# Cross attention over 256 keys: the tail of one more quad deferred, one copy reordered, one batch's loads a slot later

## The chip, the core and the metric

The kernel runs on one core of one Trainium2 chip. The metric is the device time of one execution in microseconds (us). All times below are of the kernel before the change, unless said otherwise.

## The reference

Eight batches of 256 tokens, 1024 features, 32 heads of 32. `x` is normalised, projected to queries, attends to 256 context rows that serve as keys and values without a projection, and the result is projected and added to `x`:

```python
mu, var = mean(x), var(x)                          # over the 1024 features
xn = (x - mu) * rsqrt(var + 1e-5) * ln_gamma + ln_beta
Q = split_heads(xn @ Wq.T)                         # (8, 32, 256, 32)
K = V = split_heads(ctx)                           # (8, 32, 256, 32)
probs = softmax(where(mask, Q @ K.T * 32**-0.5, -inf))
out = x + merge_heads(probs @ V) @ Wout.T
```

All arithmetic is in 32-bit floats.

## The kernel before

The work is cut into 64 **quads**: a quad is four heads of one batch, so quad n is heads 4(n % 8) to 4(n % 8) + 3 of batch n // 8. The main loop (L905) has one **slot** n per quad. In slot n TensorE (PE) does, in this order: the scores of quad n + 1 (`scores`, L471, 16 matmuls), the weighted sum of values of quad n - 2 (`values`, L614, 64 small matmuls), query projections for quads to come (`make_q`, L331, into one PSUM bank; from slot 18 on `query_product`), and steps of the output projection of the batch before (`product_steps`, L681). The order of all this is written out by hand: instructions are issued to every engine in program order.

`softmax_parts` (L491), called in slot n for quad n + 1, does the softmax of four heads. `exps(j)` takes minimum and exponential of head j (VectorE, then ScalarE), `normalize(j)` divides (VectorE and GpSimd), `blocks(j)` transposes 32 x 32 blocks into the tile `pT` (VectorE), and `aside` copies parts of `pT` to `pc` (ScalarE). What is left then is the **tail** (L595): `blocks(3)`, `aside(1)`, two transfers `pT<-pT` of 128 KB (L600), then the loads listed in `between`, and then two transfers `pT<-pc` (L604). The last two overwrite what the first two read, so each waits for the landing of its partner. `values` of the quad needs all four. The tail is either issued at once or put in the list `tails`; then the next softmax issues it behind its own `exps(0)` (L555). L608 decides which: quads below 8, and quads 57 to 62, are put in the list.

All these transfers go through SyncE's queue (SP), which issues them in program order; an issue takes 0.5 to 0.6 us. Each carries one of eight completion semaphores in turn (100 to 105, 107 and 108 in the trace's operands) and waits, before it is issued, until the transfer eight places earlier has landed.

Behind the softmax, slot n issues the rest of its list: layer norm steps, and `move_x` (L316 to L327), which carries the normalised and block-transposed `x` of a batch from tile `xe` to tile `xnT` in sixteen transfers of 64 KB. For batch 2 the moves lie in slots 5 (four), 6 (six) and 7 (six), and the first reader is `make_q` of quad 16 in slot 10.

The table of slots (L790 to L816): for batch 3 (`SPLIT`), `first` is 18, so its `x` is loaded (two halves of 512 KB) in the lists of slots 5 and 6, its statistics (`ln_stats`, L216) lie in slots 8 and 9, its normalisation in 10 and 11. A load in the list of slot n goes out with the tail of quad n + 1. Statistics of slots up to 8 are used to fill gaps in the softmax; later ones come behind it.

Before the main loop, quad 0 is done by hand (L851 to L882): its query projection in two halves of tokens, `first_q(0)` and `first_q(1)` (each eight chunks of matmuls and one ScalarE copy, L289), the scores of each half, and `softmax_parts(0, ...)` as a generator that is advanced between them.

Of the kernel before, what the change touches and what calls it, by code (L numbers as in the profile page):

```python
# [59 lines left out]
def xattn_kernel(  # L60
# [16 lines left out]
    NQ = NC  # L77
    NH = P // HD
# [8 lines left out]
    N = B * NQ  # L87
# [191 lines left out]
    def first_q(s, chunks=range(NC)):  # L279

        if s == 0:
            pqs[0] = ps_q.tile([P, 512], F32, tag="pq", name="pq_0")
        cols = ds(0, P) if s == 0 else ds(P, P + 1)
        for c in chunks:
            nc.tensor.matmul(
                pqs[0][:, cols], wq[:, 0, c, :], xnT0[:, c, cols],
                start=(c == chunks[0]), stop=(c == chunks[-1]),
            )
        nc.scalar.activation(qa[:, 0, cols], pqs[0][:, cols], AF.Copy, scale=NEG_SCALE)  # L289
# [83 lines left out]
    SPLIT = 3  # L373
# [110 lines left out]
    def softmax(*args):  # L484
        for _ in softmax_parts(*args):
            pass
# [4 lines left out]
    def softmax_parts(n, copies=(), ahead=(), between=(), hooks={}, fill=()):  # L491

        fill = list(fill)

        def fill_in():
            if fill:  # L500
                fill.pop(0)()

        pss = scs[n]
        pT = pTs[n] = ptp.tile([P, 2, NI, NH, NS, K], F32, tag="pT", name=f"pT_{n}")
        pc = asp.tile([P, NI, NH, NS, K], F32, tag="pc", name=f"pc_{n}")
        es, mns, dens = {}, {}, {}

        def exps(j, part=range(NS)):
            if 0 in part:
                es[j] = ep.tile([P, NS, T], F32, tag="e", name=f"e_{n}_{j}")  # L510
                mns[j] = sm.tile([P, NS], F32, tag="mn", name=f"mn_{n}_{j}")
                dens[j] = sm.tile([P, NS], F32, tag="den", name=f"den_{n}_{j}")
            e, mn, den = es[j], mns[j], dens[j]
            for s in part:
                nc.vector.tensor_tensor_reduce(  # L515
                    out=e[:, s, :], in0=pss[j][:, s, :], in1=mbs[n // NQ], scale=1.0,
                    scalar=NO_SCORE, op0=ALU.add, op1=ALU.min, accum_out=mn[:, s : s + 1],
                )
                nc.scalar.activation(  # L519
                    e[:, s, :], e[:, s, :], AF.Exp, bias=mn[:, s : s + 1], scale=-1.0,  # L520
                    accum_out=den[:, s : s + 1],
                )

        def normalize(j):
            rden = sm.tile([P, NS], F32, tag="rden", name=f"rden_{n}_{j}")
            nc.vector.reciprocal(rden, dens[j])  # L526
            for s in range(NS):
                nc.gpsimd.tensor_scalar(  # L528
                    es[j][:, s, :], es[j][:, s, :], rden[:, s : s + 1], 1.0,
                    ALU.mult, ALU.mult,  # L530
                )

        def blocks(j):
            nc.vector.transpose(  # L534
                pT[:, :, :, j, :, :].rearrange("p a i s k -> p (a i) s k"),
                es[j].rearrange("p s (b t) -> p b s t", t=K),
            )

        def aside(j):
            nc.scalar.copy(pc[:, :, ts(j, 2)], pT[:, 1, :, ts(j, 2)])  # L540

        if n == 0:
            for j in range(NH - 1):
                exps(j, (0,))
            yield
            exps(NH - 1, (0,))
            fill_in()
            yield
            for j in range(NH):
                exps(j, (1,))  # L550
            normalize(0)
            fill_in()
        else:
            exps(0)
            while tails:  # L555
                tails.pop()()
            late = "p1" in hooks
            if not late:
                for done in list(pvs):
                    copy_at(done)  # L560
            exps(1)
            for hook in hooks.get("soon", ()):
                hook()
            exps(2)
            normalize(0)
            for hook in hooks.get("p1", ()):
                hook()
            exps(3)
            if late:
                for done in list(pvs):  # L570
                    copy_at(done)
        copies = list(copies)
        for copy in copies[: NQ if n <= NQ else 1 if n == NQ + 1 else 0]:
            copies.remove(copy)
            copy()
        for hook in hooks.get(0, ()):
            hook()
        normalize(1)
        fill_in()
        blocks(0)  # L580
        for hook in hooks.get(1, ()):
            hook()
        normalize(2)
        fill_in()
        blocks(1)
        aside(0)
        normalize(3)
        fill_in()
        blocks(2)
        while fill:  # L590
            fill_in()
        for copy in copies:
            copy()

        def tail():  # L595
            blocks(3)
            aside(1)

            for r in range(2):
                nc.sync.dma_start(pT[ts(2 * r, K), 1], pT[ts(2 * r + 1, K), 0])  # L600
            for load in between:
                load()
            for r in range(2):
                nc.sync.dma_start(pT[ts(2 * r + 1, K), 0], pc[ts(2 * r, K)])  # L604

        for load in ahead:
            load()
        if n < NQ or N - NQ < n < N - 1:  # L608
            tails.append(tail)
        else:  # L610
            tail()
        yield
# [16 lines left out]
    def copy_at(n):  # L629
        b, c = divmod(n, NQ)  # L630
        k, c = divmod(c, NK)
        if c == 0:
            ats[b, k] = atp.tile([P, NK, NS, NA, K], F32, tag="at", name=f"at_{b}_{k}")
        for r, pv in enumerate(pvs.pop(n)):
            nc.scalar.copy(  # L635
                ats[b, k][:, c, :, ts(r, 2), :], pv.rearrange("p a s k -> p s a k")
            )
# [136 lines left out]
    for n in range(N):  # L774
# [12 lines left out]
    loads, stats, norms, trans, moves, biases, masks = (  # L787
        {n: [] for n in range(N)} for _ in range(7)
    )
    for b in range(1, B):  # L790
        first = NQ * (b - 1) + 2
        if b == 1:
            when = dict(moves=())
        elif b == 2:
            when = dict(
                loads=(0, 1), stats=(2, 3), norms=(3, 3), trans=(4, 5),
                moves=tuple(5 + (i + 2) // 6 for i in range(16)),
            )
        else:
            when = dict(  # L800
                loads=(first - 13, first - 12),
                stats=(first - 10, first - 9) if b == SPLIT else (first - 11, first - 9),
                norms=(first - 8, first - 7), trans=(first - 7, first - 6),
                moves=tuple(first - 6 + (i + 2) // 6 for i in range(16)),
            )
        for table, key in (
            (loads, "loads"), (stats, "stats"), (norms, "norms"), (trans, "trans"),
        ):
            for i, n in enumerate(when.get(key, ())):
                assert n < first  # L810
                table[n].append((b, i))
        for n in range(N):
            part = [i for i, slot in enumerate(when["moves"]) if slot == n]
            if part:
                assert n < first - 1
                moves[n].append((b, part))  # L816
        biases[NQ * b - 2].append(b)
        if b % 2 == 0:
            masks[NQ * b - 7].append(b)
# [47 lines left out]
    for c in range(NC):  # L867
        copy_x0(1, c, nc.scalar if c < NC // 2 else nc.vector)
    first = softmax_parts(0, (partial(copy_q, 1), partial(copy_q, 2)), (), (), {}, [
        partial(ln_stats, 1, 0), partial(ln_stats, 1, 1),  # L870
        partial(ln_norm, 1, 0, nc.vector),
    ])
    next(first)
    first_q(1)
    make_q(1, second=True, chunks=range(2))
    next(first)
# [9 lines left out]
    for b in range(B - 1):  # L886
        done, ends = 0, b == B - 2
        for i, counts in enumerate(ENDS if ends else STEPS):
            n = NQ * (b + 1) + i
# [15 lines left out]
    for n in range(N):  # L905
        b, i = divmod(n - NQ, NQ)
# [222 lines left out]
```

## Time and profile before

| | us |
|---|---|
| median of 3 runs | 575.77 (575.03 to 577.52) |
| the profiled execution, its own time | 575.24 |
| its span, first to last instruction | 573.5 |
| PE busy in it | 565.9 (99%), granted clock 0.999 |
| VectorE (DVE), ScalarE (ACT), GpSimd (POOL) busy | 459.2, 412.3, 403.8 (80%, 72%, 70%) |
| transfers: bytes moved, mean rate | 117.98 MB, 206 GB/s |

The slots around the change, with the start of their scores on PE as borders (busy us of each engine, and the mean busy share of the 16 DMA engines):

| slot | from, to | length | PE | DVE | ACT | POOL | DMA |
|---|---|---|---|---|---|---|---|
| 6 | 65.30, 73.33 | 8.03 | 8.03 | 6.88 | 6.80 | 7.70 | 0.95 |
| 7 | 73.33, 80.87 | 7.54 | 7.54 | 6.79 | 6.37 | 7.45 | 0.81 |
| 8 | 80.87, 89.68 | 8.81 | 7.96 | 8.07 | 6.76 | 8.15 | 0.78 |
| 9 | 89.68, 98.24 | 8.56 | 8.56 | 5.71 | 6.66 | 7.61 | 0.77 |
| 10 | 98.24, 109.04 | 10.80 | 8.69 | 8.67 | 6.87 | 9.61 | 0.60 |
| 11 | 109.04, 118.29 | 9.25 | 9.25 | 7.08 | 6.96 | 6.13 | 0.86 |

In the profile's lines, times are us from the span's start; a line of the timeline gives start, length, engine, line of the kernel, operation, output <- inputs, shapes and count, and in brackets how long the engine was idle before and what ended that.

### The profile page before, as it was taken

What the parts mean: (1) busy time and instruction counts of PE and PEld (TensorE: products, weight loads), DVE (VectorE), ACT (ScalarE), POOL (GpSimd) and SP (SyncE); (2) the same over time, 40 slices, a digit from 0 to 9 for tenths busy, and PEclk for the clock granted to TensorE, in tenths of its full rate; (3) what the DMA queues carried; (4) which work ended last, traced back from release to release, by engine and by line L of the source; (5) the groups of instructions that cost most, each with busy time, mean ns of one, the idle gap of its engine ahead of it and who ended that gap; (6) DMA issues with size and microseconds to landing.
All of it is one profiled execution on the core that took longest, in us unless ns stands there. A gap on an engine that the chain in (4) does not pass through costs nothing.

```text
span 573.5 us, 20000 instructions
## 1 busy us (share of the span) xinstructions
PE 565.9 (99%) x7162; PEld 392.1 (68%) x7162; DVE 459.2 (80%) x1698; ACT 412.3 (72%) x1424; POOL 403.8 (70%) x675
## 2 busy tenths in 40 slices
PE   8999999899999999999999999999999999999997
PEld 8788876566667677677676677667766777755444
DVE  6897987788877879888888888888877868879823
ACT  4688886767758867698667967769767876869920
POOL 1788898789896896776567675666657667448780
PEclk9999999999999999999999999999999999999999
DMA  8675877766678667877787767886768774536751
GB/s 299 238 201 189 241 216 216 240 186 189 192 239 273 195 181 220 248 241 204 202 239 208 214 196 192 251 263 190 181 177 258 210 228 141 142 101 180 212 162 74
DMA packets 47475, 117.98 MB, mean 206 GB/s; under 512 B 9104, under 2 KB 9872, under 8 KB 47376
## 3 DMA queue, kind: packets, MB, share of 16 engines
q1 hardware_dynamic: 47088, 116.69, 68.9%
q8 instruction: 57, 0.93, 0.7%
q14 instruction: 42, 0.34, 0.2%
q10 hardware_dynamic: 288, 0.01, 0.0%
HBM read 65.28 MB, written 11.53 MB: 134 GB/s over the span
## 4 chain that ended last, share of the span: by engine, by line
PE 86%; POOL 4%; DVE 4%; DMA 2%; ACT 1%; issue 1%; SPq 1%; DVEq 0%; ACTq 0%; POOLq 0%
PE po_S L694 20%; PE pq_A L440 16%; PE pv L622 11%; PE sc L479 10%; PE po_A L694 10%; PE pq L340 7%; PE pq_S L440 6%; PE po_end L761 3%; POOL e L528 3%; DVE e L515 2%; DMA pT<-pT 1%; PE po_last L761 1%; ACT e L519 1%; PE busy L120 1%; DVE pT L534 1%
## 5 line engine op out<-in xcount | busy, mean ns | idle before, releaser
L528 POOL TENSOR_SCALAR e<-e,rden 128x256 f32<-128x256 f32 x512 | 235.8, 478 | 128.7 <-DVE rden L526 127.0
L519 ACT ACTIVATE e<-e,mn 128x256 f32<-128x256 f32 x512 | 254.1, 501 | 51.2 <-DVE mn L515 50.8
L534 DVE STREAM_TRANSPOSE pT<-e 128x512 f32<-128x512 f32 x256 | 180.7, 707 | 53.1 <-POOL e L528 35.5
L515 DVE CUSTOM_DVE_ANT_0 e<-sc,mb 128x256 f32<-128x256 f32 x512 | 185.9, 416 | 26.9 <-PE sc L479 26.4
L540 ACT COPY pc<-pT 128x512 f32<-128x512 f32 x128 | 79.0, 617 | 68.7 <-DVE pT L534 41.2
L519 ACT ACTIVATION_READ_ACCUMULATOR e<-e,mn 128x1 f32 x512 | 97.9, 191 | 0.0
L340 PE MATMUL pq<-xnT,wq 128*128 128x256 f32 (+1 forms) x368 | 84.2, 383 | 2.1 <-DMA xnT<-xe 2.1
L340 PEld LDWEIGHTS pq<-xnT,wq 128*128 128x128 f32 x368 | 68.6, 190 | 16.8 <-issue 6.9
L622 PE MATMUL pv<-pT,v 64*32 64x128 f32 x4096 | 74.8, 274 | 1.0 <-issue 0.8
L622 PEld LDWEIGHTS pv<-pT,v 64*32 64x32 f32 x4096 | 57.1, 105 | 26.7 <-issue 12.7
L479 PEld LDWEIGHTS sc<-k,qa 32*128 32x128 f32 x1024 | 46.2, 184 | 42.4 <-issue 23.2
L694 PE MATMUL po_S<-wo,at 128*128 128x512 f32 x152 | 74.3, 606 | 0.0
L479 PE MATMUL sc<-k,qa 32*128 32x256 f32 x1024 | 73.6, 400 | 0.1
L694 PE MATMUL po_A<-wo,at 128*128 128x512 f32 x128 | 60.9, 609 | 0.0
L694 PE MATMUL po_S<-wo,s 128*128 128x512 f32 x104 | 50.1, 606 | 0.0
L526 DVE RECIPROCAL rden<-den 128x2 f32<-128x2 f32 x256 | 37.6, 147 | 6.0 <-ACT e L519 4.8
L515 DVE DVE_READ_ACCUMULATOR2_ANT mn<- 128x1 f32 x512 | 42.4, 83 | 0.0
L440 PEld LDWEIGHTS pq_A<-xnT,wq 128*128 128x128 f32 x320 | 37.3, 192 | 4.8 <-issue 4.1
L694 PEld LDWEIGHTS po_A<-wo,at 128*128 128x128 f32 x128 | 22.5, 189 | 24.6 <-issue 22.7
L694 PEld LDWEIGHTS po_S<-wo,at 128*128 128x128 f32 x152 | 25.8, 190 | 19.8 <-issue 19.1
L440 PE MATMUL pq_A<-xnT,wq 128*128 128x128 f32 x320 | 37.3, 275 | 0.0
L635 ACT COPY at<-pv 128x128 f32<-128x128 f32 x128 | 26.2, 254 | 8.2 <-PE pv L622 8.2
(95 smaller groups left out, 605.1 us busy)
## 6 DMA issues: line engine op xcount, KB each, us to landing
v<-in_kv_dram SPq DMA_DIRECT2D x32, 512.0 KB, 4.4
pT<-pT SPq DMA_DIRECT2D x128, 128.0 KB, 2.9
pT<-pc SPq DMA_DIRECT2D x128, 128.0 KB, 4.1
ring<-kept_T SPq DMA_DIRECT2D x18, 512.0 KB, 5.3
k<-in_kv_dram SPq DMA_DIRECT2D x32, 256.0 KB, 3.7
x<-in_x_dram SPq DMA_DIRECT2D x14, 512.0 KB, 5.6
r<-in_x_dram SPq DMA_DIRECT2D x28, 256.0 KB, 5.1
out_dram<-r SPq DMA_DIRECT2D x28, 256.0 KB, 2.5
```

Source lines behind the costliest of these rows:

```text
L340: nc.tensor.matmul(pqs[n], wq[:, o, c, :], xnTs[b](c), start=(c == 0), stop=(c == NC - 1),)
L440: nc.tensor.matmul(pqs[b][:, o, :], w[:, c], x_[:, c], start=begins and o + c == 0, stop=c == NK - 1, skip_group_check=True,)
L479: nc.tensor.matmul(scs[n][j][:, s, :], qa[r, n % NQ, ts(s, P)], ks[n - n % 2][r, n % 2, :], start=True, stop=True,)
L515: nc.vector.tensor_tensor_reduce(out=e[:, s, :], in0=pss[j][:, s, :], in1=mbs[n // NQ], scale=1.0, scalar=NO_SCORE, op0=ALU.add, op1=ALU.m ...
L519: nc.scalar.activation(e[:, s, :], e[:, s, :], AF.Exp, bias=mn[:, s : s + 1], scale=-1.0, accum_out=den[:, s : s + 1],)
L526: nc.vector.reciprocal(rden, dens[j])
L528: nc.gpsimd.tensor_scalar(es[j][:, s, :], es[j][:, s, :], rden[:, s : s + 1], 1.0, ALU.mult, ALU.mult,)
L534: nc.vector.transpose(pT[:, :, :, j, :, :].rearrange("p a i s k -> p (a i) s k"), es[j].rearrange("p s (b t) -> p b s t", t=K),)
L540: nc.scalar.copy(pc[:, :, ts(j, 2)], pT[:, 1, :, ts(j, 2)])
L622: nc.tensor.matmul(pvs[n][r][j * HD : (j + 1) * HD], vs[n - n % 2][ts(r, 2 * K), i, ds(n % 2 * P + j * HD, HD)], pT[ts(r, 2 * K), :, i, j, ...
L635: nc.scalar.copy(ats[b, k][:, c, :, ts(r, 2), :], pv.rearrange("p a s k -> p s a k"))
L694: nc.tensor.matmul(po, operand(b, name)[:, c], wo[:, which, c], start=begins and c == 0, stop=c == NK - 1, skip_group_check=not begins,)
```

## The change

Three edits.

- In `softmax_parts` for quad 0, all four heads' first halves are now issued in one part, and the caller no longer advances the generator before `first_q(1)`. So `first_q(1)`, whose ScalarE copy was issued behind three exponentials, and the two first chunks of `make_q(1)` are now issued ahead of all four.
- L608: `n < NQ` becomes `n <= NQ` (NQ is 8). The tail of quad 8 is issued within the softmax of quad 9, behind its `exps(0)`. What slot 7 has behind the softmax, the last six moves of batch 2 among it, is thereby issued ahead of this tail.
- Batch 3's `x` goes from the lists of slots 5 and 6 into those of 6 and 7, and its statistics from slots 8 and 9 to 9 and 10.

```diff
         if n == 0:
-            for j in range(NH - 1):
+            for j in range(NH):
                 exps(j, (0,))
-            yield
-            exps(NH - 1, (0,))
             fill_in()
             yield
...
-        if n < NQ or N - NQ < n < N - 1:
+        if n <= NQ or N - NQ < n < N - 1:
             tails.append(tail)
...
             when = dict(
-                loads=(first - 13, first - 12),
-                stats=(first - 10, first - 9) if b == SPLIT else (first - 11, first - 9),
+                loads=(first - 12, first - 11) if b == SPLIT else (first - 13, first - 12),
+                stats=(first - 9, first - 8) if b == SPLIT else (first - 11, first - 9),
                 norms=(first - 8, first - 7), trans=(first - 7, first - 6),
...
-    next(first)
     first_q(1)
     make_q(1, second=True, chunks=range(2))
     next(first)
```

## The prediction

> **What bounds the kernel now.** I read the page's first part, then who PE waits for, then PE's timeline slot by slot, then SP's, since the waits left on PE lead to transfers. The page and PE's waits:
>
> ```profile
> span 573.5 us, 20000 instructions
> PE 565.9 (99%) x7162; PEld 392.1 (68%) x7162; DVE 459.2 (80%) x1698; ACT 412.3 (72%) x1424; POOL 403.8 (70%) x675
> ...
> PE pq L340 <- DMA xnT<-xe: 2.1, 1, 2.1
> PE busy L120 <- POOL ring masks.py:199: 1.3, 1, 1.3
> PE pv L622 <- issue: 0.8, 2, 0.6
> ```
>
> PE is busy 99% of the span at full clock, and its waits are few and each in one place. So no edit to another engine's order can bring more than the sum of PE's few waits. PE's timeline gives their places (slots 7 to 10; a row is a block of matmuls, its first number its start):
>
> ```profile
> 73.33 1.15 PE L479 MATMUL sc<-k,qa 32*128 32x256 f32 x16
> 74.41 1.16 PE L622 MATMUL pv<-pT,v 64*32 64x128 f32 x64
> 75.49 5.45 PE L340 MATMUL pq<-xnT,wq 128*128 128x256 f32 x24
> 80.87 1.15 PE L479 MATMUL sc<-k,qa 32*128 32x256 f32 x16
> 82.58 0.38 PE L622 MATMUL pv<-pT,v 64*32 64x128 f32 x2 [0.57 <-issue]
> 83.24 1.13 PE L622 MATMUL pv<-pT,v 64*32 64x128 f32 x62 [0.28 <-issue]
> 84.30 5.45 PE L340 MATMUL pq<-xnT,wq 128*128 128x256 f32 x24
> 89.68 1.15 PE L479 MATMUL sc<-k,qa 32*128 32x256 f32 x16
> ...
> 99.32 1.22 PE L622 MATMUL pv<-pT,v 64*32 64x128 f32 x64
> 100.47 1.12 PE L694 MATMUL po_A<-wo,at 128*128 128x512 f32 x2
> 103.70 3.69 PE L340 MATMUL pq<-xnT,wq 128*128 128x256 f32 x16 [2.11 <-DMA xnT<-xe]
> ```
>
> Slots 7 and 8 hold the same 104 matmuls, yet one takes 80.87 - 73.33 = 7.54 us and the other 89.68 - 80.87 = 8.81. The difference, **1.27 us**, lies around the values of quad 6: two of them start at 82.58, the rest only at 83.24. In slot 10, the two projection matmuls of 100.47 need 0.95 (half of the 1.81 that four take between 107.23 and 109.04), but the queries of quad 16 start at 103.70: 103.70 - 101.42 = **2.28 us**, put down to the moves of batch 2.
>
> SP's queue says why (one row: so many transfers, first issue, time until the last was issued):
>
> ```profile
> 74.53 0.44 SPq L130 DMA_DIRECT2D x<-in_x_dram  x1
> 75.02 0.43 SPq L173 DMA_DIRECT2D wo<-in_woT_dram  x1
> 75.55 1.15 SPq L604 DMA_DIRECT2D pT<-pc  x2
> ...
> 85.06 0.44 SPq L130 DMA_DIRECT2D x<-in_x_dram  x1
> 85.55 0.43 SPq L173 DMA_DIRECT2D wo<-in_woT_dram  x1
> ...
> 88.57 0.57 SPq L144 DMA_DIRECT2D v<-in_kv_dram  x1
> 94.61 1.95 SPq L604 DMA_DIRECT2D pT<-pc  x2
> 96.61 3.75 SPq L327 DMA_DIRECT2D xnT<-xe  x6
> ```
>
> Quad 6's two `pT<-pc` go out at 75.55 and land at 82.50 and 83.15 by the trace's landing records: 7 us, because the loads of v (lands 77.88), x (79.44) and wo (82.18) are ahead. PE's two starts, 82.58 and 83.24, stand just behind. The last six moves go out only from 96.61 because quad 8's tail is ahead of them, whose `pT<-pc` waits on SP until 94.61 for its partner's landing.
>
> **The change, part by part.** The sum is against the profiled execution's 575.24.
>
> (A) Without x in quad 6's tail, its `pT<-pc` no longer have 512 KB ahead that took 79.44 - 77.88 = 1.56 us. They land at 80.94 and 81.59, and the values of quad 6 can start at 80.87 + 1.08 = 81.95 (as 74.41 stands to 73.33). The wait goes: **-1.27**. It is close (0.36): if wo took the 3.0 that one took behind a k load earlier (67.50 to 70.50) instead of 2.74, 0.1 would be left; if the loads do not close up, all stays. Bounds -1.27 to 0.
>
> (B) The six moves of slot 7 come ahead of quad 8's tail, about ten us earlier. Their reader at 101.42 less 1.27 finds them landed: **-2.28**. Bounds -2.28 and -2.1, the two readings.
>
> (C) What is late next is quad 8's tail itself. On SP it now stands behind the six moves, and gets the second half of x between its two pairs. VectorE's `blocks(3)` and ScalarE's `aside(1)` go behind the `exps(0)` of quad 9, some 1 us (two exponentials of 0.50): SP reaches their reader much later, so this costs nothing. Step by step: SP gives each transfer one of eight semaphores and waits for the landing eight places back. Eight places ahead of the sixth move stands the wo load of 85.55, which lands at 93.16 now, and at 91.6 if everything from (A) on is 1.56 earlier. So that move goes out at 91.6, and behind it at SP's pace of 0.6: `pT<-pT` at 92.2 and 92.8, v 93.4, x 94.0, r 94.5, `pT<-pc` 95.0 and 95.6. The v load needs 3.9 from its issue in a short queue (3.8 and 4.0 in two answers): 97.3; x 1.56 more: 98.9; r 0.66 (96.06 to 96.72 now): 99.5; the two copies some 0.3 each: 100.1. The values of quad 8 were due at 99.32 - 1.27 = 98.05. A new wait of **+2.05**, on PE ahead of the projection and of quad 16's queries, so all of PE stands behind it. No row shows this arrangement, so bounds: low, the wo load lands when most of its engines have it (91.43 now, 1.7 ahead of the last) and the loads follow at the 1.27 of the opening's 512 KB weights: 97.8, no wait, 0. High, nothing closes up and wo lands at 93.16, and one engine is held by a 1.1 us instruction fetch as at 95.11: 102.8, +4.7. I take 2.05, nearer the low end, since its terms are those of the very neighbours.
>
> Here a rule may be held against the rows. A lone 128 KB pair transfer takes 2.3 us from issue to landing, and 512 KB in a queue 1.56. The Trainium skill ("DMA: Bandwidth & Descriptors", section "Anatomy of one DMA") gives, for the other path of issue, a fixed 2.0 us plus bytes over 436 GB/s. By it the 1.5 MB from 93.4 on would be down at 98.9, an estimate from that page, and the sum 1.2 lower; the rows say slower, and I go by them.
>
> (D) The opening. The copy of quad 0's second half of queries starts at 14.73, behind three exponentials, and the scores at 15.04 wait for it (PE's weight loads 0.49). Its last matmul ends at 14.09, so it can start at 14.15 and PE, which ends its two chunks at 14.80, gains 0.25. In exchange ScalarE holds the four exponentials, the first now at 13.24, until 14.41; four of 0.495 end the issue at 16.39 where the next is free at 16.25: 0.14 late, under a later gap of 3.09 on ScalarE before 22.08. PE's 0.25 are lost again at 26.63, where the transposes of batch 1 start as GpSimd's normalisation (22.85, 3.78 long) ends; that chain hangs on VectorE, whose order is the same. **0**, bounds -0.3 and +0.2 (without that cover, 0.14 of exponentials reach quad 0's reciprocals).
>
> (E) The statistics moved, 2 x 0.67 + 0.20 + 0.15 = 1.7 us of VectorE, leave slot 8 (8.07 busy) and come to slot 10, behind its softmax. They end by 8.7 of work in a slot over 8.5 long and only delay the next `exps(0)`, whose scores buffers PE needs a slot later: **0**, bounds 0 and +0.5. Quad 7's values start at 94.38, its copies land at 93.59 and 94.09: both move by 1.3 to 1.6, cost 0, and up to 0.6 if only PE moves.
>
> Sum: 575.24 - 1.27 - 2.28 + 2.05 = **573.74**. The median shown is 0.53 above that execution, so the forecast for a median is **574.3**.
>
> **The rivals.**
>
> *The whole gain.* Quad 8's copies land by 98.05, and both waits go for nothing: 575.77 - 3.55 = 572.2. For it: the straggling engine is 1.7 of wo's landing, and the DMA share is 0.60 in slot 10. Against: three loads of 1.28 MB between the pairs.
>
> *Slower.* The wait of quad 8's values takes over both: at the high end of (C), 575.77 - 3.55 + 4.7 = 576.9. It decides against the change once the second `pT<-pc` lands after 98.05 + 3.55 = 101.6. Quad 9's tail follows on SP, and if its values in slot 11 wait 2 us as well, it is 578.9. For it: eight transfers in flight, and SP stands still until a wo load of 7.6 us is down. Against: (A) frees that load earlier.
>
> *The x load does not do what it says.* wo is the load ahead that matters, quad 6's copies stay late, (A) is 0, and (C) starts from 93.16: 101.7 - 99.32 = 2.4 against 2.28. 575.9, no change.
>
> **How the numbers follow.** Forecast 0.52 (573.2 to 575.4), whole gain 0.22, slower 0.15, no effect of x 0.11. Low end: the whole gain less the opening's bound, 572.0; high end 577.0, the slower case. A measurement here tells about 0.5%, 2.9 us: below 572.9 or above 578.7. Faster than that 0.20 (nearly all of the whole gain), slower 0.08 (the slower case with quad 9's wait), within 0.72.
>
> **What would show it.** (A) slot 8 is 7.5 long. (B) no wait of PE for the moves; they are issued by 92. (C) the values of quad 8 wait some 2 us, its copies land near 100. (D) the copy of 14.73 at 14.2, the transposes at 26.6 as before. (E) no PE wait in slots 11 and 12. I am wrong if quad 8's copies land by 98, or after 101.6.

## The result, and the profile after

| | median of the runs, us | lowest, highest | runs |
|---|---|---|---|
| before | 575.74 | 573.01, 577.75 | 20 |
| after | 578.90 | 574.86, 581.80 | 20 |

The ratio is 1.0047, 95% interval 1.0031 to 1.0063 (the two medians alone give 1.0055): the change makes the kernel slower by 0.3 to 0.6%. Two later executions of before that took 950 us at a granted clock of 0.56 are left out of all figures below. The profiled execution of after took 574.86 us (span 573.1), less than that of before (575.24). It is the fastest of the 20, and its mean granted clock is 1.000; 12 of the others have 0.994 or less, seven 0.997. In a span of 575 us, 0.997 and 0.994 are 3.4 and 6.8 us at half clock. So the first trace of after shows the change's steps, and not yet where the typical execution loses its time. Both belong to the explanation.

First the trace of after. Who PE waits for:

```profile
PE pv L620 <- DMA pT<-pT: 2.5, 1, 2.5
PE busy L120 <- POOL ring masks.py:199: 1.4, 1, 1.4
PE pq L285 <- ACT xnT L275: 0.9, 1, 0.9
PE px L266 <- DVE x L252: 0.2, 1, 0.2
```

The waits for quad 6's values and for the moves are gone, and one new wait is there: the values of quad 8 (line 622 is 620 now). The last two rows lie in the first 9 us; the kernel with x alone moved has such a wait too (0.9), and at slot 7 this trace is 0.17 behind before's (73.50 against 73.33). PE's timeline of slots 8 to 10:

```profile
81.04 1.15 PE L479 MATMUL sc<-k,qa 32*128 32x256 f32 x16
82.11 1.22 PE L620 MATMUL pv<-pT,v 64*32 64x128 f32 x64
83.26 5.45 PE L340 MATMUL pq<-xnT,wq 128*128 128x256 f32 x24
88.64 1.15 PE L479 MATMUL sc<-k,qa 32*128 32x256 f32 x16
...
97.20 1.15 PE L479 MATMUL sc<-k,qa 32*128 32x256 f32 x16
100.83 1.52 PE L620 MATMUL pv<-pT,v 64*32 64x128 f32 x64 [2.48 <-DMA pT<-pT]
102.28 1.13 PE L692 MATMUL po_A<-wo,at 128*128 128x512 f32 x2
103.25 3.62 PE L340 MATMUL pq<-xnT,wq 128*128 128x256 f32 x16
106.70 1.88 PE L692 MATMUL po_S<-wo,s 128*128 128x512 f32 x4
108.51 1.15 PE L479 MATMUL sc<-k,qa 32*128 32x256 f32 x16
```

Slot 8 is 7.60 long (8.81 before), and the queries of quad 16 follow the projection without a gap. Slot 10 is 11.31 long (10.80 before): if the 2.28 for the moves are gone, quad 8's values cost 2.79 (2.48 of them the wait ahead of their first matmuls). SP's queue (first issue of a row, time until its last) has the order that the change gives it:

```profile
84.20 1.15 SPq L602 DMA_DIRECT2D pT<-pc  x2
85.40 6.07 SPq L327 DMA_DIRECT2D xnT<-xe  x6
91.58 1.16 SPq L598 DMA_DIRECT2D pT<-pT  x2
92.78 0.58 SPq L144 DMA_DIRECT2D v<-in_kv_dram  x1
93.40 0.45 SPq L130 DMA_DIRECT2D x<-in_x_dram  x1
93.89 1.20 SPq L150 DMA_DIRECT2D r<-in_x_dram  x1
95.19 1.61 SPq L602 DMA_DIRECT2D pT<-pc  x2
```

The sixth move goes out at 90.96, when the wo load of 83.67 has landed (90.94), and quad 8's tail behind it. Its two last copies land at 100.49 and 101.13 by the landing records; PE starts on the first at 100.83.

### The profile page after: what moved, and what is told of

Read it like the earlier page. It is cut to its first block, busy times and chain, and to the rows that moved or that the text cites. A ratio compares the mean times of both kernels' runs of the same rounds, so it can differ in the third digit from the quotient of the medians.

```text
span 573.1 us, 19993 instructions
## 1 busy us (share of the span) xinstructions
PE 565.2 (99%) x7162; PEld 391.4 (68%) x7162; DVE 459.6 (80%) x1698; ACT 412.1 (72%) x1424; POOL 403.8 (70%) x675
## 4 chain that ended last, share of the span: by engine, by line
PE 85%; POOL 5%; DVE 4%; DMA 2%; ACT 2%; issue 1%; SPq 1%; ACTq 0%; POOLq 0%
PE po_S L692 20%; PE pq_A L440 16%; PE pv L620 11%; PE sc L479 10%; PE po_A L692 10%; PE pq L340 7%; PE pq_S L440 6%; POOL e L528 3%; PE po_end L759 3%; DVE e L515 1%; DMA pT<-pT 1%; PE po_last L759 1%; ACT e L519 1%; DVE pT L534 1%; DVE st L226 1%
```

## The experiments

**After once more, and each edit alone.** These four ran on one chip (before there: 576.42, 35 runs).

> The changed kernel again. Theory 'clock': the new wait of PE for quad 8's copies (2.5 us in the profile of after) is long enough that the granted clock halves for some us behind it in most executions: median near 578.7, most executions with a mean clock of 0.994 to 0.997, and if the profiled one is such, its matmuls run at half pace somewhere in 98 to 112 us and nowhere else. Rival 'opening': the half pace lies in the first 30 us. Rival 'transfers': clock 0.999 to 1.000 throughout, and the wait itself is 5 to 7 us.

Measured: 578.79, ratio 1.005 (1.0027 to 1.0072); of its 12 executions one at clock 1.000 (575.27), three at 0.997, eight at 0.994. The profiled one (span 579.7) is of the common kind. PE's timeline of slot 10, and three stretches of it (length, busy time of PE, PEld, DVE, ACT, POOL, then the granted clock, DMA share and GB/s):

```profile
97.88 1.15 PE L479 MATMUL sc<-k,qa 32*128 32x256 f32 x16
105.33 2.08 PE L620 MATMUL pv<-pT,v 64*32 64x128 f32 x64 [6.30 <-DMA pT<-pc]
107.33 2.07 PE L692 MATMUL po_A<-wo,at 128*128 128x512 f32 x2
109.20 4.36 PE L340 MATMUL pq<-xnT,wq 128*128 128x256 f32 x16
113.39 1.88 PE L692 MATMUL po_S<-wo,s 128*128 128x512 f32 x4
115.20 1.15 PE L479 MATMUL sc<-k,qa 32*128 32x256 f32 x16
```

```profile
88.00:103.87 15.87, 11.02 (x116) 5.70 (x115) 10.75 (x40) 9.49 (x31) 13.33 (x19) 1.00 0.87 219
103.87:110.70 6.83, 5.38 (x70) 3.72 (x71) 1.25 (x4) 1.55 (x7) 0.00 (x0) 0.50 0.48 110
110.70:125.00 14.30, 14.30 (x131) 9.54 (x134) 12.49 (x44) 10.79 (x34) 12.16 (x23) 1.00 0.75 242
```

Both theories hold, each for a part. The wait is 6.30 instead of 2.48, and the clock stands at half from 103.87 to 110.70: the values' 64 matmuls take 2.00 to the next start instead of 1.45, the two projection matmuls 1.87 instead of 0.97. The spans differ by 6.6: 3.82 for the longer wait (105.33 - 97.88 against 100.83 - 97.20), 2.19 for the half clock (115.20 - 105.33 against 108.51 - 100.83), and 0.68 from ahead of slot 10. From its first rise at 4.88 (4.51 in after) to 103.87 the clock is full: the opening is not the place.

> Only the tail of quad 8 deferred. x stays in slots 5 and 6, so quad 6's wait (1.27) stays, the wait for the moves (2.28) goes, and quad 8's copies have 512 KB less ahead: a wait of 0.5 to 1.0. 'Clock': no wait reaches 2 us, so clocks of 0.999 and more, 574.0 to 574.8, about 0.998 of before. 'Opening': the same. 'Transfers': a wait of 2 us or more stays in slot 10, 575.5 to 577.

```diff
-        if n < NQ or N - NQ < n < N - 1:
+        if n <= NQ or N - NQ < n < N - 1:
```

Measured: 577.42, ratio 1.0026 (1.0004 to 1.0049); ten of 12 executions below 0.999. Above all three bands. The profiled execution (span 578.2) has lost nothing to the moves, 0.78 to quad 8's values, 1.05 to quad 5's, and 3.1 to quad 6's values, which x in the lists of slots 5 and 6 holds up as before, only longer; the clock stands at half for 3.41 us behind that.

```profile
85.62 0.38 PE L622 MATMUL pv<-pT,v 64*32 64x128 f32 x2 [1.56 <-ACT e L519]
87.56 1.57 PE L622 MATMUL pv<-pT,v 64*32 64x128 f32 x62 [1.57 <-issue]
```

So the deferral alone is a loss, just clear of noise, though it removes the wait for the moves. Where it loses, this trace does not show: quad 6's copies go out at 77.40 and 78.01, and the first transfers that the deferral puts in another place only at 90.89.

> Only the opening reordered. 'Clock' and 'transfers': as before, 575.7, ratio 0.999 to 1.001. 'Opening': 577.5 to 579, ratio 1.003 to 1.006, with a lower mean clock than the kernel before on the same chip.

```diff
-            for j in range(NH - 1):
+            for j in range(NH):
                 exps(j, (0,))
-            yield
-            exps(NH - 1, (0,))
...
-    next(first)
     first_q(1)
```

Measured: 576.68, ratio 1.0011 (0.999 to 1.0032). The opening does nothing that can be told. Its trace shows something else: it has the kernel before's wait for the moves, and here the clock falls behind it.

```profile
103.84 5.38 PE L340 MATMUL pq<-xnT,wq 128*128 128x256 f32 x16 [2.14 <-DMA xnT<-xe]
```

```profile
105.02:108.43 3.41, 3.41 (x10) 2.70 (x9) 2.88 (x6) 1.30 (x5) 3.41 (x8) 0.50 0.81 224
```

The queries of quad 16 take 5.38 instead of 3.69, after nearly the same wait as in before's trace (2.11, no fall). The kernel before has such executions too: of the 91 that ran beside these experiments, 47 have a clock of 0.999 or more (median 575.71), 41 about 0.997 (577.18).

> Only batch 3's x a slot later. Quad 6's wait goes (-1.27); the second half of x now stands in quad 8's tail ahead of its copies, and behind them the six moves: PE's wait for the moves grows from 2.28 to 4 to 5 us. 'Clock': one wait of over 2.5 us, mean clocks below 0.998, 577 to 580. 'Opening': clocks as before, 575.7 to 577. 'Transfers': 576 to 577, clock 0.999.

```diff
-                loads=(first - 13, first - 12),
-                stats=(first - 10, first - 9) if b == SPLIT else (first - 11, first - 9),
+                loads=(first - 12, first - 11) if b == SPLIT else (first - 13, first - 12),
+                stats=(first - 9, first - 8) if b == SPLIT else (first - 11, first - 9),
```

Measured: 572.96, ratio 0.9955 (0.9934 to 0.9976), 11 of 12 executions at clock 0.999 or more. All theories were wrong, that of the clock the most (577 to 580): it is the fastest of the four. PE's slot 10 and SP's queue in its trace:

```profile
97.18 1.15 PE L479 MATMUL sc<-k,qa 32*128 32x256 f32 x16
98.26 1.48 PE L622 MATMUL pv<-pT,v 64*32 64x128 f32 x64
99.66 1.12 PE L694 MATMUL po_A<-wo,at 128*128 128x512 f32 x2
100.62 3.62 PE L340 MATMUL pq<-xnT,wq 128*128 128x256 f32 x16
```

```profile
84.33 1.15 SPq L604 DMA_DIRECT2D pT<-pc  x2
85.58 1.18 SPq L600 DMA_DIRECT2D pT<-pT  x2
86.81 0.58 SPq L144 DMA_DIRECT2D v<-in_kv_dram  x1
87.43 0.46 SPq L130 DMA_DIRECT2D x<-in_x_dram  x1
87.93 0.54 SPq L150 DMA_DIRECT2D r<-in_x_dram  x1
93.01 1.15 SPq L604 DMA_DIRECT2D pT<-pc  x2
94.21 4.56 SPq L327 DMA_DIRECT2D xnT<-xe  x6
```

Here both old waits are gone, and no new one is there. Quad 8's `pT<-pT` go out at 85.58, six us ahead of after's 91.58, since they need not stand behind a move that needs the wo load's semaphore. The second x load is in the queue early, and quad 8's copies land at 98.12 and 98.47, some 0.3 late for their values. The six moves go out from 94.21, 2.4 ahead of before, because everything on SP is earlier since quad 6's tail; the last lands at 100.24, its reader starts at 100.62.

**Without the deferral, and with only its effect on SP undone.** These four ran on a second chip (before there: 576.73, 29 runs).

> Opening and batch 3's x moved, the tail of quad 8 not deferred. If the opening does nothing and the x loads alone bring the gain: 572.7 to 573.3, as with x alone, ratio 0.995, clocks 1.000. If the opening costs something: 573.5 to 575.

Its edit is the opening's and the loads' of above. Measured: 573.44 (6 runs), ratio 0.9949 (0.9934 to 0.9965), all clocks 1.000. Against after, it lacks the deferral alone: that single line is the loss, 1.0047 against 0.9949.

> The changed kernel, tail of quad 8 deferred, but with the six moves of slot 7 behind its transfers again, so SP has the order of the kernel without the deferral, while VectorE and ScalarE keep the deferred order. Theory 'order on SP': the loss of the deferral is gone, 572.7 to 573.5, clocks 1.000, no wait in slot 10 above 0.6 us. Rival 'the deferral itself' (blocks and copies of quad 8 later on VectorE and ScalarE): 576 to 579, wait for quad 8's copies stays at 2 us or more.

```diff
                 nc.sync.dma_start(pT[ts(2 * r + 1, K), 0], pc[ts(2 * r, K)])
+            if n == NQ:
+                for args in moves[NQ - 1]:
+                    move_x(*args)
...
-        for args in moves[n]:
+        for args in moves[n] if n != NQ - 1 else ():
             move_x(*args)
```

Measured: 573.88, ratio 0.9961 (0.9944 to 0.9979); ten of 12 at clock 1.000. With the deferral kept on VectorE and ScalarE, putting the six moves behind the tail again brings back nearly all. So the loss comes from the order on SP. The profiled execution (span 573.6, slower than its median) shows how narrow the other order is as well: its moves go out from 96.30, and PE waits for them again.

```profile
103.77 3.69 PE L340 MATMUL pq<-xnT,wq 128*128 128x256 f32 x16 [1.72 <-DMA xnT<-xe]
```

> The changed kernel with the second half of batch 3's x in the list of slot 8 instead of 7: quad 8's copies have the moves ahead on SP, but 512 KB less between the pairs. Theory: their landing comes 1.6 us earlier or more, the wait is 1 to 2.5, the clock falls in about half of the executions: 574.5 to 577. If the moves alone made the wait and the load did nothing: 578 to 579 as after.

```diff
-                loads=(first - 12, first - 11) if b == SPLIT else (first - 13, first - 12),
+                loads=(first - 12, first - 10) if b == SPLIT else (first - 13, first - 12),
```

Measured: 575.15, ratio 0.9988 (0.997 to 1.0007); eight of 12 at clock 0.999 or more. The profiled execution, the fastest of the 12, waits 0.57 for quad 8's values. As the theory had it: the moves and the 512 KB between the pairs share the blame for the wait.

> The changed kernel plus 12 matmuls of no use (128 x 128 x 128, 24 instructions, some 2.7 us at full clock) ahead of quad 8's values, into the bank that the values overwrite: more work, the same wait for the copies. Theory 'clock': PE stands still for shorter, the clock falls less often or for one window instead of two, and the time falls by 1 to 2.5 us against after: 576 to 577.8. Rival, the half clock is only a mark of executions whose transfers are slow and costs nothing of itself: the time stays at 578.5 to 579 or rises by up to 0.5.

```diff
+        for _ in range(extra):
+            nc.tensor.matmul(
+                pvs[n][0].rearrange("p a s k -> p (a s k)"), wq[:, NC - 1, 0, :], wq[:, NC - 1, 1, :],
+                start=True, stop=True,
+            )
         for i in range(NI):
...
-            values(n - 2)
+            values(n - 2, 12 if n == NQ + 2 else 0)
```

Measured: 576.82, ratio 1.0014 (0.9994 to 1.0034); nine of 12 executions keep a clock of 1.000 (median 576.27), against two of after's 32. More work on PE and a shorter time, by 0.36% or some 2 us against the 1.0050 of the changed kernel, where the rival had no gain at all: the half clock costs by itself. How much is known only roughly, since the two ran on different chips and their intervals just overlap. The profiled execution is one of the three others: even with the 24 instructions the wait goes on for 2.45, and the clock halves at 104.43.

```profile
99.13 2.94 PE L618 MATMUL pv<-wq 128*128 128x128 f32 x24
104.53 2.53 PE L625 MATMUL pv<-pT,v 64*32 64x128 f32 x64 [2.45 <-issue]
```

**The opening within the change, and x still later.** These three ran on a third chip (before there: 576.98, 27 runs).

> The changed kernel with the opening as before. If the opening plays no part: as after, ratio 1.004 to 1.006, clocks of 0.994 to 0.997. If the reordered opening brings GpSimd's and PE's order out of step and so makes the wait longer: 575.5 to 577, clocks of 1.000 in half.

Its edit is after's without the opening. Measured: 578.32, ratio 1.0034 (1.0015 to 1.0052), six executions each at 0.994 and 0.997. The opening plays no part that can be told. The profiled wait for quad 8's copies is 3.6, and the clock stands at half for 6.83 us from 100.31, before the wait ends.

```profile
101.54 2.13 PE L622 MATMUL pv<-pT,v 64*32 64x128 f32 x64 [3.61 <-DMA pT<-pc]
```

> The kernel before with batch 3's x in slots 6 and 8, no other edit: quad 6's tail is free of x, and quad 8's copies and the six moves behind them have 512 KB less ahead than with slots 6 and 7. Theory 'order on SP': the moves land 1.5 us earlier, the remaining wait of quad 8's values (0.4) goes: 572.3 to 573.0, no slower than x in 6 and 7 on the same chip. Rival: the load is only pushed into the tail of quad 9, whose values wait instead: 573.5 to 575.

Its edit is the one line of the loads with slots 6 and 8, without deferral and opening. Measured: 575.26, ratio 0.9983 (0.9958 to 1.0008). A miss: slower than x in slots 6 and 7, and not for the rival's reason. No wait for quad 9's values; PE waits for the moves again.

```profile
PE pq L340 <- DMA xnT<-xe: 2.0, 1, 2.0
```

In this execution the moves go out from 95.74, 1.5 later than with x in 6 and 7. Of that, 1.2 is there when quad 7's `pT<-pT` go out (82.65 against 81.48), and up to there the two kernels give SP the same order; so that part is not the edit's. Whether most executions are late in this way stays open.

The last two moves land at 103.03 and 103.19, after 3.5 and 3.1 us, where the two before took 2.0. Each transfer is spread over 16 engines, and 15 of them had delivered by 101.53 and 102.12; only the last was late. A 16 KB instruction fetch of 1.18 us had begun at 100.79. All four traces in which PE waits some 2 us for the moves look like this: in before the last move's sixteenth engine delivers at 103.46 and the other 15 by 101.81, with a fetch of 1.53 from 100.88; with the opening alone 103.60 and 102.28 (1.33 from 101.00), with SP's order restored 103.53 and 102.29 (1.10 from 101.37). So 1.1 to 1.7 of each such wait is one late engine and only the rest is the order on SP. That the fetch is what held the engine fits the times; the traces do not name the engine, so it is not shown.

> Batch 3's x in slots 6 and 7 alone, again, beside the kernel with slots 6 and 8: 572.8 to 573.4, ratio 0.995.

Measured: 572.99, ratio 0.9946 (0.9919 to 0.9973). Moving the loads alone beats both kernels, twice.

## Why the prediction was wrong

The forecast was 574.3 in 572.0 to 577.0; it is 578.9.

- (A) was right: slot 8 lost 1.21 of the 1.27. Quad 6's copies landed at 80.20 and 80.64.
- (B) was right in size and wrong in its cause. The 2.28 went, but x alone removes it too: the 1.56 that I used to move quad 8's transfers forward also moves the six moves forward, by 2.4 with the deferral absent. I gave the gain to the deferral without asking what the other edit had left of that wait. I also read the whole 2.28 as SP's order, where before's trace has 15 of the 16 engines done by 101.81 and one at 103.46; with x alone the last move is down at 100.24, ahead of the next fetch (100.60). So the deferral had next to nothing to bring, only (C) to cost.
- **(C) is the step that failed, by its size.** The mechanism came as told, link by link: wo's landing 90.94 (91.6 told), the sixth move at 90.96, `pT<-pT` at 91.58 (92.2), v down at 97.28 (97.3), x at 98.77 (98.9), the copies at 101.13 (100.1), a wait of 2.48 (2.05). That was the mildest execution, and even there the last 1.1 is one engine: 15 of 16 had the last copy down by 100.00. In the three traces with the deferral and with x where the change puts it the wait is 2.48, 3.61 and 6.30, and what the sum left out altogether is what a wait of that length does to PE's clock: half pace for 6.83 us, 2.19 us lost in the trace with 6.30. In that trace the x load between the pairs needed 8.4 us (95.39 to 103.79) where I took 4.9: twelve of its 16 engines had delivered by 100.71, the last two at 103.50 and 103.79. The one instruction fetch there (1.1 us from 95.42) accounts for one engine at most; what held the other isn't known.
- The high bound of (C), 4.7, gave 576.9. It was built from lateness of transfers alone. With 6.30 and the clock it would have been 6.3 + 2.2 - 3.55 = 5.0 above before, 580.7; measured executions reach 581.8.
- The slower rival was the right one, with its place and its deciding point (a landing after 101.6: 105.32 in the second trace). It got 0.15, since I took a single execution's transfer times as typical. Quad 9's values, its further mishap, did not wait, so that its 578.9 is also the measured time is chance.
- The rule weighed at (C), the Trainium skill's fixed time plus bytes over 436 GB/s for the other path of issue ("DMA: Bandwidth & Descriptors", "Anatomy of one DMA"), gave an estimate of 98.9 for the landing; the traces have 101.13 and 105.32. The rows were the better guide, and still too kind.
- (D) was right as far as can be told: the copy starts at 14.28, the transposes at 26.63 as before, ratio 1.0011 with an interval across 1. (E) was right: the slot behind is free of waits.
- The rival in which moving x does nothing fell by the two runs of x alone.

## What to carry to other kernels

Before a gain is given to one edit, apply the other edits first and ask what is left of the wait. A transfer that is moved ahead of others on a queue with a fixed number in flight carries its own waits with it: here six small moves took quad 8's tail with them behind a 512 KB load. Where PE is the bound, a single wait of 2 us or more may cost more than its length: look at the granted clock of many executions, not of one trace. And before a late landing is put down to the order of a queue, look at when each of its 16 engines delivered.

## What the runs showed of the hardware

The granted clock goes in steps. Every stretch at half pace within the work of these traces is 3.41 or 6.83 us long, and the falls come 81.92, 95.57 and 98.99 us after the first rise of the clock, which is 24, 28 and 29 times 3.413: a grid, wherever the wait lies. Whether the clock falls goes, in these traces, with how much of one such window PE stood still, as told by the end of the last matmul and the start of the next: 40% with x in slots 6 and 8, 51% in after and in the kernel with SP's order restored, 55% in before, no fall; 63% (the opening alone), 69% (with the added matmuls), 70% (the change without the opening), 75% (the deferral alone, two waits together) and 100% (after once more), a fall at the window's end. The ends of the traces, behind PE's last matmul, fit: 45% (after once more) brought no fall, 60% (the change with x in slot 8) did. So nearly the same wait of 2.1 us brought a fall with the opening alone and none in before, by where the grid lay. In the two traces with 6.83 us at half, PE was busy for 57 and 64% of the first half-pace window, and the clock stayed at half for another.

The Trainium skill ("TensorE: Matmul & The Clock Gate", "Part 1: The HAM clock gate") speaks of a free-running window of about 3.4 us, which the traces bear out, and of an idle window as what halves the clock; here 60% of one sufficed.
